# Two transformer layers with mixtures of experts on one core: last experts as riders with late sums, the first part's first four pairs of tiles beside the last convolution, rows and sorts given out sooner

## The chip, the cores and the metric

The kernel runs on one core of a Trainium2 chip, in float32. A core has five engines, each with its own queue of instructions: PE (matrix products), DVE (vector), ACT (scalar with an activation function), POOL (here mostly the issuer of indirect transfers) and SP (issuer of plain transfers). The metric is the device time of one execution, in microseconds (us). The kernel before took 1086.53 us, the median of four runs of 1083.31 to 1088.84.

## The reference

The input x has 4 batches of 1024 rows of 256 features. Two layers follow one another, each of them an attention and a feed-forward part, with a layer norm that is scaled and shifted per batch before both and a gate per batch and feature behind both:

```
h = layernorm(x) * (1 + ca) + sa ;  x = x + ga * attention(h)
h = layernorm(x) * (1 + cb) + sb ;  x = x + gb * feed_forward(h)
```

Layer 0 has a causal softmax attention over a latent of 64 and a feed-forward part of 16 experts, of which each row takes its best two. This change leaves that layer alone. Layer 1 has a linear attention and a feed-forward part of 8 experts:

```
q, k, v = relu(h Wq)+eps, relu(h Wk)+eps, h Wv      # 16 heads of 16, q and k normalised, cubed, normalised
out     = q (k^T v) / (q . sum of k + eps)
y       = out + conv3(out)                          # three taps along the rows, per feature
attention    = y Wproj + b
feed_forward = gate_prob * (h We[e] + be[e]),  e = argmax(h Wr + br)   # one expert for each row
```

## The kernel before

All of x stays on chip. Layer 1 is what matters here.

**attention1** (L1445) walks over b = 0 to 4. In step b it runs `front(b)` beside `back(b-1)`, two generators that are advanced in turn. `front` does the layer norm of batch b, then the products for k and v (L1511), the sums of k and v (ps_kv), and the products for q (L1537). `back` does, for the batch before, the outputs ps_o (L1574), their division by the sums (DVE, L1580), their transposes ps_oT (L1589, copied to `o` by ACT, L1592), the convolution y (one ACT instruction L1597 and two of DVE, L1601, for each half of the features) and the projection ps_pr (L1609, 32 products), which DVE adds to x (L1614). I call these steps stage 0 to stage 4; stage 4 has only `back(3)`.

**Tasks and riders.** `Around` (L34) holds work that is slipped in between. A task is a generator cut into pieces; `step(pieces, rides)` advances the first task by so many pieces and the first rider so many times. A rider is a string of indirect transfers that POOL issues. `attention1` calls `step` after every turn, with a pace of (6, 8, 6, 6, 12) sixths of a piece by stage and one ride. When a stage has ended, `after_batch(b - 1)` appends the tasks of that batch's second half of the layer:

- `rows(b)` (L1827): row statistics, then `routed_rows` (L1017): normalised rows h (ACT, L1030, eight instructions of 128x256; for batches 0 and 1 DVE scales and shifts them, L1045 and L1046), stored to memory (`rows_in`, SP, L1048), transposed (ps_lnT, PE L1057), copied as hT (ACT, L1063 or L1068), and multiplied with the router (L794, L802).
- `sort(p)` (L1846): the best expert of each row, and a counting sort of the rows by expert: ranks on PE (ps_rank, L895), a chain of small DVE instructions, ps_expert (L949), index (L933) and offset (L950). It ends with a new rider, `send(p)` (L1863): rows are fetched (POOL, L1870) and scattered by their index into `sorted1` in memory (POOL, L964).

The rows are sorted in three parts, `PARTS = ((0, 1), (2,), (3,))`: batches 0 and 1 together, then batch 2, then batch 3. An expert's rows are padded to tiles of 128, so the parts have 11, 7 and 7 pairs of tiles.

**Experts1.run** (L1883) walks over these 25 pairs once attention1 has ended. For each it loads two tiles (`xs`, SP L1008, up to five pairs ahead, 256 KB each), transposes them (ps_xT, PE L1923), copies them to `xT` (ACT, L1927 for part 0; for parts 1 and 2 two instructions that also scale and shift, L1930), multiplies with the expert's weights (ps_y, PE L1938, 8 products), adds the bias (DVE, L1944, twice), for parts 1 and 2 multiplies with the gate (DVE, L1946), and stores (`results`, SP L1947). The transposes of a pair are given out ahead of the products of the pair before it. After each pair it calls `step(2, 2)`.

**combine(p)** (L1975) becomes a task when the last pair of its part is given out: it gathers the rows back (`ys`, POOL L974, 128 KB each, six buffers, four ahead), multiplies them with the router's probability and adds them to x: for part 0 with ACT (`out`, L2002), then the gate and the sum on DVE (L2007, L2008); for parts 1 and 2 with one DVE instruction (L1996). Every four tiles a store of 512 KB leaves (L2010).

**Sums.** `count_sums` (L501, four DVE instructions for each of three tensors, L495 to L498) and `out_of_bounds` (L511) check that the attentions' sums were in range, and run before the end of part 1 and of part 2; a general version of the kernel follows behind that check and isn't run here.

**The order of the instructions.** Each engine runs its instructions in the order in which they stand in its queue. Between the points where the program pins that order (`k.pin`), a scheduler chooses it when the kernel is built. ACT's normalised rows (L1030) and outputs of part 0 (L2002) are pinned; the transposes and copies of the experts are not.

Of the kernel before, what the change touches and what calls it, by code (L numbers as in the profile page):

```python
# [15 lines left out]
P = 128  # L16
B, N, C = 4, 1024, 256
NT = N // P
CC = C // P
# [481 lines left out]
def count_sums(k, pool):  # L501

    recs = [k.recs.rearrange("p n i j -> p (n i j)")]
    recs += [k.recs1[:, i].rearrange("p b t h -> p (b t h)") for i in range(2)]
    inverse = 1.0 / SUM_HI, 1.0 / SUM_LO
    for i, (rec, (low, high)) in enumerate(zip(recs, (inverse, (SUM_LO, SUM_HI), inverse))):
        good = pool.tile([P, 8 * B * H], F32, tag="xs", name="good", bufs=6)
        count_within(k, good, rec, low, high, k.good[:, i : i + 1])

# [507 lines left out]
def routed_rows(k, work, b, statistics, scale, shift, wr, br, ne, logits, scalar):  # L1017
# [33 lines left out]
    h = yield from normalised(0)  # L1051
    for q in range(2):
        hT = work.tile([P, CC, 512], F32, tag="hT", name="hT", bufs=1)
        for cc in range(CC):
# [14 lines left out]
            if q == 0 and cc == CC - 1:  # L1069
                h = yield from normalised(1)  # L1070
            else:
                yield 1
# [372 lines left out]
def attention1(ctx, k, a, after_batch=lambda b: None):  # L1445
# [171 lines left out]
    k.misc = ps_m  # L1617
    for b in range(B + 1):
        while b == HB and k.awaited in k.around.tasks:
            k.around.step()  # L1620
        todo = ([front(b)] if b < B else []) + ([back(b - 1)] if b else [])
        pace = (6, 8, 6, 6, 12)[b]
        n = 0
        while todo:
            todo = [g for g in todo if next(g, k) is not k]
            n += pace
            k.around.step(n // 6)
            n %= 6
        if b:
            after_batch(b - 1)  # L1630
# [153 lines left out]
class Experts1:  # L1784


    def __init__(self, k, a, out):
# [19 lines left out]
        self.sent = set()  # L1807
# [74 lines left out]

    def run(self, early):  # L1883

        k = self.k
        nc = k.nc
        work = self.back = self.stack.enter_context(
            k.tc.tile_pool(name="f1_work", bufs=2, reuse_waits="tile")
        )
        ps_x = self.stack.enter_context(  # L1890
            k.tc.tile_pool(name="f1_ps_x", bufs=4, space=PSUM, reuse_waits="tile")
        )
        ps_o = self.stack.enter_context(
            k.tc.tile_pool(name="f1_ps_o", bufs=4, space=PSUM, reuse_waits="tile")
        )
        k.misc = ps_x

        pairs = [
            (p, list(range(g, min(g + 2, s.tiles))))
            for p, s in enumerate(self.sortings)  # L1900
            for g in range(0, s.tiles, 2)
        ]
        coming = []

        def fetch(n):

            for p, tiles in pairs[n + len(coming) : n + 5]:
                if p not in self.sent:
                    break
                xs = work.tile([P, 2, C], F32, tag="xs", name="xs", bufs=6)  # L1910
                k.sorted1[p].load(xs[:, : len(tiles)], tiles)
                coming.append(xs)

        def tiles_of(p, tiles, xs):

            n = len(tiles)
            at = self.sortings[p].offsets(
                self.state[p][1], tiles, [mybir.EngineType.PE, mybir.EngineType.DVE]
            )
            ps = ps_x.tile([P, 2, CC, P], F32, tag="m", name="ps_xT")  # L1920
            for j in range(n):
                for cc in range(CC):
                    nc.tensor.transpose(ps[:, j, cc], xs[:, j, cc * P : (cc + 1) * P], k.ident)  # L1923
            xT = work.tile([P, 2, CC, P], F32, tag="xT", name="xT", bufs=3)
            b = PARTS[p][0] if len(PARTS[p]) == 1 else None
            if b is None:
                nc.scalar.copy(xT[:, :n], ps[:, :n])  # L1927
            else:
                for cc in range(CC):
                    nc.scalar.activation(  # L1930
                        xT[:, :n, cc], ps[:, :n, cc], AF.Identity,
                        bias=k.modF[:, cc, b : b + 1], scale=k.modF[:, 2 + cc, b : b + 1],
                    )
            yield
            po = ps_o.tile([P, 2, C], F32, tag="o", name="ps_y")
            for j in range(n):
                for cc in range(CC):
                    k.anchor = nc.tensor.matmul(  # L1938
                        po[:, j], lhsT=xT[:, j, cc], rhs=self.we[:, cc, bass.ds(at[j], C)],
                        start=cc == 0, stop=cc == CC - 1,  # L1940
                    ).ins
            y = work.tile([P, 2, C], F32, tag="y", name="y", bufs=3)
            for j in range(n):
                nc.vector.tensor_tensor(y[:, j], po[:, j], self.be[:, bass.ds(at[j], C)], ALU.add)  # L1944
            if b is not None:
                nc.vector.tensor_tensor(y[:, :n], y[:, :n], bcast(self.gate[:, b], 1, n), ALU.mult)  # L1946
            nc.sync.dma_start(k.results1[p].part(tiles), y[:, :n])  # L1947

        again, before = None, None
        for n, (p, tiles) in enumerate(pairs):  # L1950
            if p not in self.sent and before is not None:
                next(before, None)
                before = None
            while p not in self.sent:
                k.around.step(1, 2)
            fetch(n)
            now = tiles_of(p, tiles, coming.pop(0))
            next(now)
            if before is not None:
                next(before, None)  # L1960
            before = now
            if n + 1 == len(pairs) or pairs[n + 1][0] != p:
                next(before, None)
                before = None
                if early and p + 2 == len(PARTS):
                    count_sums(k, work)
                if early and p + 1 == len(PARTS):
                    again = out_of_bounds(k, work, ps_x)
                k.around.tasks.append(self.combine(p))
            k.around.step(2, 2)  # L1970
        k.around.drain()
        self.stack.close()
        return again

    def combine(self, p):  # L1975
        k, work = self.k, self.back
        nc = k.nc
        index, _, part = self.state[p]
        most = self.sortings[p].nt

        def fetch(n):
            ys = work.tile([P, C], F32, tag="ys", name="ys", bufs=6)
            self.sortings[p].gather(ys, k.results1[p], index[:, 0, n : n + 1])
            return ys

        coming = []
        for n in range(4):
            coming.append(fetch(n))
            yield 0.5
        for n in range(most):  # L1990
            j = n % 2
            b, t = PARTS[p][n // NT], n % NT
            ys = coming.pop(0)
# [9 lines left out]
            if n + 4 < most:  # L2003
                coming.append(fetch(n + 4))
            if j == 1 and len(PARTS[p]) > 1:
                xs = k.x[b][:, t - 1 : t + 1]
                nc.vector.tensor_tensor(y, y, bcast(self.gate[:, b], 1, 2), ALU.mult)  # L2007
# [10 lines left out]
def two_layers(ctx: ExitStack, tc: tile.TileContext, a: dict, out: bass.AP):  # L2018
# [56 lines left out]
    def stages(first, second, early):  # L2075
# [22 lines left out]
        with ExitStack() as s, tc.using_default_side("right"):  # L2098
# [3 lines left out]
            second(s, k, a, *([after_attention1] if early else []))  # L2102
# [84 lines left out]
```

## The time and the profile before

| | us |
| --- | --- |
| time, median of 4 runs | 1086.53 (1083.31 to 1088.84) |
| the profiled execution | 1090.69, its span 1088.9 |
| PE busy | 951.6 (87%) |
| DVE busy | 620.5 (57%) |
| ACT busy | 602.8 (55%) |
| POOL busy | 336.9 (31%) |
| mean granted clock of PE | 0.950 |

Times within the profile count from the start of the span. The marks that are used below, all from the timeline of PE: the last q product of batch 2 ends at 887.6, that of batch 3 at 939.9; the last ps_pr ends at 972.2; the last ps_y at 1062.7. Layer 1's experts so fill the last 117 of 1088.9 us. In a table by stretches each engine's busy time stands as "busy (xinstructions)"; the two figures behind are the clock that PE was granted, as a share of full speed, the share of the 16 DMA engines' time that is busy, and GB/s. A bracket behind an instruction gives the idle time before it and what ended it.

### The profile page before, as it was taken

How to read it: one execution, taken by the hardware profiler on the slowest of the kernel's cores; microseconds unless marked ns; L12 is line 12 of the kernel's file. 1: busy time of each engine (PE TensorE's matmuls, PEld its weight loads, DVE VectorE, ACT ScalarE, POOL GpSimd, SP SyncE). 2: the span in 40 equal slices, each digit the busy share in tenths (PEclk: the TensorE clock that was granted, in tenths of full speed). 3: DMA queues.
4: the chain of work that ended last, by engine and by line, in shares of the span. 5: the costliest groups of instructions: out<-in, count | busy, mean ns of one | idle time of the engine just before them, and what ended most of it. 6: DMA issues, size and time to landing. Idle time of an engine off the chain costs nothing.

```text
span 1088.9 us, 18090 instructions
## 1 busy us (share of the span) xinstructions
PE 951.6 (87%) x6072; PEld 564.6 (52%) x6072; DVE 620.5 (57%) x1987; ACT 602.8 (55%) x959; POOL 336.9 (31%) x528
## 2 busy tenths in 40 slices
PE   4899999999999999889689999986997989858770
PEld 1434434343443434335567888874465656546650
DVE  5822335422465155414676757993899978664572
ACT  0358754765477555675555666766654745523430
POOL 2013111311222234673004615612550100553632
PEclk9999999999999999999899999998999899989875
DMA  6995000100010001552824656624223201458764
GB/s 196 352 346 192 2 1 6 40 1 1 2 64 1 1 30 54 196 225 75 313 88 163 198 181 187 195 76 144 65 65 148 88 1 39 139 172 258 234 214 129
DMA packets 97142, 132.89 MB, mean 122 GB/s; under 512 B 8536, under 2 KB 84216, under 8 KB 96528
## 3 DMA queue, kind: packets, MB, share of 16 engines
q1 hardware_dynamic: 84656, 97.27, 26.5%
q0 software_dynamic: 11776, 33.57, 9.9%
q8 instruction: 52, 0.85, 0.3%
q10 hardware_dynamic: 608, 0.79, 0.2%
q14 instruction: 50, 0.41, 0.1%
HBM read 67.85 MB, written 63.75 MB: 121 GB/s over the span
## 4 chain that ended last, share of the span: by engine, by line
PE 64%; DVE 18%; DMA 5%; issue 5%; ACT 4%; POOL 1%; SPq 1%; DVEq 0%; ACTq 0%; POOLq 0%
PE ps_s L388 13%; PE ps_av L453 12%; PE ps_qk L364 5%; PE ps_y L1312 5%; PE ps_h L1247 5%; PE ps_v L349 3%; PE ps_out L427 3%; PE ps_pr L1609 3%; PE ps_k L1511 2%; PE ps_q L1537 2%; PE ps_y L1938 2%; DMA ys<-results,index 2%; DVE y L1601 2%; PE ps_lnT L1057 1%; PE ps_xT L1224 1%
## 5 line engine op out<-in xcount | busy, mean ns | idle before, releaser
L396 ACT ACTIVATE pT<-ps_s 128x1024 f32<-128x1024 f32 x288 | 279.3, 1022 | 168.6 <-PE ps_s L388 166.2
L399 POOL TENSOR_SCALAR_AFFINE_SELECT pT<-pT 128x256 f32<-128x256 f32 x256 | 104.0, 430 | 329.7 <-ACT pT L396 325.0
L388 PE MATMUL ps_s<-qT,kT 32*128 32x512 f32 (+3 forms) x1536 | 178.6, 522 | 0.1
L453 PE MATMUL ps_av<-pT,v 128*32 128x512 f32 (+3 forms) x1536 | 166.1, 500 | 8.3 <-DVE turned L411 5.6
L964 POOL DMA_INDIRECT sorted<-hs,index x96 | 97.3, 1013 | 146.1 <-PE ps_y L1312 74.1
L974 POOL DMA_INDIRECT ys<-results,index x96 | 102.8, 1070 | 119.5 <-DMA results<-y 43.6
L388 PEld LDWEIGHTS ps_s<-qT,kT 32*128 32x128 f32 x1536 | 74.3, 184 | 96.0 <-issue 73.4
L453 PEld LDWEIGHTS ps_av<-pT,v 128*32 128x32 f32 x1536 | 40.8, 109 | 103.1 <-issue 59.1
L1247 PE MATMUL ps_h<-w,xT 128*128 x352 | 83.5, 391 | 6.9 <-DVE mv L1259 3.8
L1312 PE MATMUL ps_y<-w,act 128*128 x352 | 84.1, 393 | 4.1 <-DVE rs_seed L84 2.8
L411 DVE STREAM_TRANSPOSE turned<-ps_av 128x512 f32<-128x512 f32 x32 | 22.8, 712 | 97.8 <-PE ps_av L453 97.5
L1247 PEld LDWEIGHTS ps_h<-w,xT 128*128 128x128 f32 x352 | 67.4, 197 | 16.7 <-issue 4.2
L1312 PEld LDWEIGHTS ps_y<-w,act 128*128 128x128 f32 x352 | 67.9, 198 | 14.0 <-ACT act L1295 4.7
L1295 ACT ACTIVATE act<-ps_hT,gain 128x128 f32<-128x128 f32 x176 | 63.6, 462 | 17.0 <-PE ps_hT L1286 17.0
L1270 ACT ACTIVATE hid<-hid,nmr,rstd 128x256 f32<-128x256 f32 x88 | 47.5, 603 | 39.7 <-DVE nmr L1263 39.5
L1938 PE MATMUL ps_y<-we,xT 128*128 x200 | 55.3, 426 | 12.0 <-ACT xT L1930 9.4
L1511 PE MATMUL ps_k<-wqkv,hT 128*128 128x512 f32 x128 | 62.2, 605 | 3.9 <-DMA wqkv<-in_wqkv_dram 3.2
L371 DVE COPY qT<-ps_qk 128x512 f32<-128x512 f32 x16 | 11.0, 690 | 81.3 <-PE ps_qk L364 81.3
L1938 PEld LDWEIGHTS ps_y<-we,xT 128*128 128x128 f32 x200 | 39.7, 211 | 21.8 <-ACT xT L1930 12.2
L103 DVE BATCH_NORM_STATS2 ln_st<-x 128x6 f32<-128x256 f32 x128 | 49.2, 407 | 0.4
L1255 DVE TENSOR_TENSOR hid<-ps_h,b 128x256 f32<-128x256 f32 x88 | 33.9, 415 | 27.4 <-PE ps_h L1247 15.8
L374 DVE TENSOR_SCALAR kT<-ps_qk,par 128x512 f32<-128x512 f32 x32 | 22.5, 745 | 38.1 <-PE ps_qk L364 38.1
(223 smaller groups left out, 1503.0 us busy)
## 6 DMA issues: line engine op xcount, KB each, us to landing
xs<-sorted SPq DMA_DIRECT2D x69, 256.0 KB, 3.7
results<-y SPq DMA_DIRECT2D x69, 256.0 KB, 2.5
sorted<-zero SPq DMA_DIRECT2D x2, 6016.0 KB
rows_in<-h SPq DMA_DIRECT2D x16, 512.0 KB, 4.3
hs<-rows_in POOLq DMA_DIRECT2D x32, 256.0 KB, 3.4
w<-in_w_dram SPq DMA_DIRECT2D x8, 1024.0 KB, 9.8
x<-in_x_dram SPq DMA_DIRECT2D x4, 1024.0 KB, 7.5
b<-in_b_dram SPq DMA_DIRECT2D x2, 2048.0 KB, 16.9
```

The costliest lines, as they stand in the source:

```text
L364: nc.tensor.matmul(ps, lhsT=w[:, cc, g * P : (g + 1) * P], rhs=hT[:, cc, hf * 512 : (hf + 1) * 512], start=cc == 0, stop=cc == CC - 1,)
L388: k.anchor = nc.tensor.matmul(pair[hh // 2][:, hh % 2, c0 : c0 + w], lhsT=kTs[o][rows, kb * P : (kb + 1) * P], rhs=qT[rows, q1 - w : q1], ...
L396: nc.scalar.activation(pT, ps, AF.Exp, scale=1.0 / L**0.5)
L399: nc.gpsimd.affine_select(out=pT[:, :, c0 : c0 + P], in_=pT[:, :, c0 : c0 + P], compare_op=ALU.is_ge, fill=0.0, base=0, pattern=[[0, 2], [ ...
L453: nc.tensor.matmul(po[32 * hh : 32 * hh + 32, 512 - w :], lhsT=vs[b % 2][:, kb, 8 * g + 2 * hh + o, :], rhs=exps[b, g, o, u][hh // 2][:, h ...
L964: i = self.k.nc.gpsimd.indirect_dma_start(out=buffer.ap, out_offset=bass.IndirectOffsetOnAxis(ap=index, axis=0), in_=rows, in_offset=None, ...
L974: self.paced(self.k.nc.gpsimd.indirect_dma_start(out=rows, out_offset=None, in_=buffer.ap, in_offset=bass.IndirectOffsetOnAxis(ap=index, a ...
L1247: mm = nc.tensor.matmul(ph[:, j], lhsT=xTs[i // 2][:, j, cc], rhs=w1[:, cc, bass.ds(at[i + j], C)], start=cc == 0, stop=cc == CC - 1,)
L1295: o = nc.scalar.activation(act[:, j, cc], pt[:, j, cc], AF.Gelu, bias=gain[:, 1, cc, t : t + 1], scale=gain[:, 0, cc, t : t + 1],)
L1312: mm = nc.tensor.matmul(po[:, j], lhsT=acts[i // 2][:, j, cc], rhs=w2[:, cc, bass.ds(at[i + j], C)], start=cc == 0, stop=cc == CC - 1,)
L1511: k.anchor = nc.tensor.matmul(ps, lhsT=hT[:, cc, t * P : (t + 1) * P], rhs=wqkv[:, cc, C:], start=cc == 0, stop=cc == CC - 1,).ins
L1938: k.anchor = nc.tensor.matmul(po[:, j], lhsT=xT[:, j, cc], rhs=self.we[:, cc, bass.ds(at[j], C)], start=cc == 0, stop=cc == CC - 1,).ins
```

## The change

- `attention1` calls `after_batch(b - 1)` when `back(b - 1)` has run out, and no longer at the end of the stage; the pace of stage 3 is 8 for 6; stages 3 and 4 have two rides for each step.
- `routed_rows` normalises both halves of a batch ahead of the first transposes, for batches 2 and 3 (those without `scale`).
- In stage 4 a new call, `fill(turn)`, runs `Experts1.beside`: pairs 0 to 3 of part 0 are fetched from turn 1 on and given out at turns 6, 7 and 8, between the transposes and the convolution and the projection of the last batch. Their buffers are cut from two spare tiles, and their banks of PSUM are the attention's.
- `run` begins at pair 4. It steps four pieces after each pair until part 2 has been sent, then two. The gathers of each part are a rider (`gathers`, with 24 buffers for 6) that is appended as soon as the part's last pair has been given out. `combine(0)` becomes a task when part 1's last pair has been given out; `combine(1)` and `combine(2)` come after all gathers have been issued.
- `count_sums` is given out in three pieces behind pairs 7, 8 and 9, from another buffer; `out_of_bounds` comes behind the last pair.
- The first transpose, the copies and the first product of each pair are pinned, and so is the gate of part 0's outputs.

The core of the diff:

```diff
     for i, (rec, (low, high)) in enumerate(zip(recs, (inverse, (SUM_LO, SUM_HI), inverse))):
-        good = pool.tile([P, 8 * B * H], F32, tag="xs", name="good", bufs=6)
+        good = pool.tile([P, 8 * B * H], F32, tag="out", name="good")
         count_within(k, good, rec, low, high, k.good[:, i : i + 1])
+        yield
...
     h = yield from normalised(0)
+    second = (yield from normalised(1)) if scale is None else None
...
             if q == 0 and cc == CC - 1:
-                h = yield from normalised(1)
+                if second is None:
+                    h = yield from normalised(1)
+                else:
+                    h = second
+                    yield 1
...
-        todo = ([front(b)] if b < B else []) + ([back(b - 1)] if b else [])
-        pace = (6, 8, 6, 6, 12)[b]
+        behind = back(b - 1) if b else None
+        todo = ([front(b)] if b < B else []) + ([behind] if b else [])
+        pace = (6, 8, 6, 8, 12)[b]
         n = 0
+        turn = 0
         while todo:
             todo = [g for g in todo if next(g, k) is not k]
+            if behind is not None and behind not in todo:
+                behind = None
+                after_batch(b - 1)
             n += pace
-            k.around.step(n // 6)
+            k.around.step(n // 6, 1 + b // (B - 1))
             n %= 6
-        if b:
-            after_batch(b - 1)
+            turn += 1
+            if b == B:
+                fill(turn)
...
+    def beside(self, turn):
+        if 0 not in self.sent or turn > 8:
+            return
...
+            self.space, self.most = space, 4
+        self.fetch()
+        for _ in range({6: 2, 7: 1, 8: 1}.get(turn, 0)):
+            self.pair()
+        if turn == 8:
+            self.products()
...
+        while self.done < len(self.pairs):
+            p = self.pairs[self.done][0]
+            if p not in self.sent:
+                self.products()
             while p not in self.sent:
-                k.around.step(1, 2)
...
+                around.step(1, 2)
+            self.pair()
+            if p == 0 and self.done > 6:
+                next(counts, None)
+            if self.done == len(self.pairs) or self.pairs[self.done][0] != p:
+                around.riders.append(self.gathers(p))
+                if p == last - 1:
+                    around.tasks.append(self.combine(0))
+            around.step(2 if last in self.sent else 4, 2)
+        for _ in counts:
+            pass
+        again = out_of_bounds(k, work, ps_x) if early else None
+        while around.riders:
+            around.step(0)
+        around.tasks += [self.combine(p) for p in range(1, last + 1)]
+        around.drain()
...
+    def gathers(self, p):
+        index = self.state[p][0]
+        for n in range(self.sortings[p].nt):
+            ys = self.back.tile([P, C], F32, tag="ys", name="ys", bufs=24)
+            self.sortings[p].gather(ys, self.k.results1[p], index[:, 0, n : n + 1])
+            self.got[p].append(ys)
+            yield
```

As built, the queues of both kernels are the same up to the last q product of batch 1 (at about 830 us). From there on the order on PE is, in the kernel after: in stage 2 the first transposes of `rows(0)` stand beside ps_o of `back(1)`; in stage 3 the ranks of `sort(0)` stand early in the k products, `rows(2)` among the later k and the q products, with the eight h and then the first two hT in one block on ACT, and the ranks of `sort(1)` between the last q product and ps_o of `back(3)`. Stage 4 reads ps_xT 0, ps_xT 1, ps_o, ps_oT, ps_o, ps_oT, ps_y 0, ps_xT 2, ps_y 1, ps_xT 3, ps_y 2, ps_y 3, and then all of ps_pr. Behind it come ps_xT 4, half of `rows(3)`, ps_xT 5, ps_y 4, the other half, ps_xT 6, ps_y 5, the ranks of `sort(2)`, and pairs 6 to 24.

## The prediction, written before the run

> **What bounds the kernel now.** I read the page's head first (PE is busy 87% of the span), then the table by stretches of layer 1, then the chain that ended last, then the waits of ACT and the timelines there. The stretches show where PE's 87% has holes:
>
> ```profile
> core 0: us, PE busy (x) PEld busy (x) DVE busy (x) ACT busy (x) POOL busy (x), PEclk, DMA share, GB/s
> 888.00:909.00 21.00, 15.36 (x92) 10.89 (x91) 15.18 (x28) 13.34 (x23) 0.00 (x0) 0.92 0.14 50
> ...
> 940.00:972.00 32.00, 19.57 (x135) 15.87 (x135) 20.43 (x71) 12.62 (x21) 18.32 (x19) 0.84 0.57 189
> 972.00:997.00 25.00, 20.38 (x135) 15.47 (x134) 11.43 (x52) 10.99 (x20) 8.90 (x11) 1.00 0.74 236
> 997.00:1018.00 21.00, 19.56 (x107) 16.37 (x106) 9.30 (x31) 6.32 (x12) 11.09 (x11) 1.00 0.81 263
> 1018.00:1047.00 29.00, 19.82 (x73) 15.17 (x72) 21.69 (x42) 14.16 (x30) 18.33 (x18) 0.76 0.67 210
> 1047.00:1063.00 16.00, 12.13 (x47) 9.39 (x45) 10.80 (x26) 2.97 (x6) 4.91 (x5) 0.79 0.63 200
> ```
>
> PE is full at 997 to 1018 alone (19.56 of 21 us, full clock). Stage 4 (940 to 972) leaves it 12.4 us idle, the stretch from 1018 to 1047 9.2, and in both the granted clock falls (0.84, 0.76). The chain names who holds it up:
>
> ```profile
> 963.40 8.81 PE ps_pr L1609 x32
> ...
> 1015.56 4.83 DMA ys<-results,index
> 1021.06 3.69 DMA ys<-results,index
> 1024.77 0.51 ACT out L2002
> 1025.28 0.46 ACT xT L1930
> ...
> 1046.71 5.61 DMA xs<-sorted
> ```
>
> The end hangs on part 0's gathers: ACT's queue has `out` (waiting for a gathered tile) ahead of `xT` (which PE waits for). The waits of ACT, and the group of the products with PE's idle time, measure it:
>
> ```profile
> ACT out L2002 <- DMA ys<-results,index: 14.0, 12, 3.0
> ```
>
> ```profile
> L1938 PE MATMUL ps_y<-we,xT 128*128 x56 | 18.8, 490 | 9.2 <-ACT xT L1930 9.2
> ```
>
> The timeline of PE gives the prices: a warm pair, two behind idle time, one with the wait of a sort, one with late rows.
>
> ```profile
> 897.73 0.63 PE L1057 MATMUL ps_lnT<-ident,h 128*128 128x128 f32 x4 [3.60 <-DVE h L1046]
> ...
> 963.19 0.20 PE L949 MATMUL ps_expert<-past,all 8*1 8x14 f32 x2 [7.51 <-DVE index L933]
> ...
> 1016.48 1.89 PE L1938 MATMUL ps_y<-we,xT 128*128 x8
> ...
> 1031.19 2.02 PE L1938 MATMUL ps_y<-we,xT 128*128 x8 [1.75 <-ACT xT L1930]
> ...
> 1052.45 2.02 PE L1923 MATMUL ps_xT<-ident,xs 128*128 128x128 f32 x8 [3.27 <-DMA xs<-sorted]
> 1054.72 3.75 PE L1938 MATMUL ps_y<-we,xT 128*128 x8 [0.25 <-ACT xT L1930]
> ```
>
> A warm pair costs PE 1.73 us (the chain's eight products) + 0.44 (four transposes) = 2.17; between 999 and 1018 pairs follow each other every 2.2 to 2.3.
>
> **The change part by part.** I walk four marks: A, the last q of batch 2 (887.6); B, that of batch 3 (939.9); C, the last ps_pr (972.2); D, the last ps_y (1062.7); then the end, 1088.9.
>
> *Stage 2, A.* `rows(1)`'s PE work moves in from stage 3: 16 transposes, routes and logits, 2.2 us. The second block of four h (2.07 on ACT) and its hT now stand ahead of `back(1)`'s copies o, so convolution and ps_pr come 2.8 later, and one k tile less stands before ps_pr to fill (2.2). Sum +7.2. Bounds: 0 (PE idles before ps_pr anyway) to 7.2, as all three are then open; I take the upper end, since the built order leaves only two k tiles as cover. A = 894.8.
>
> *Stage 3, B.* Away: `rows(1)`'s 2.2, the idle 5.6 of 888 to 909 (3.60 of it the row above), about 1.0 of slow clock (0.92). Added: the ranks of `sort(0)` stand right behind the last q, and ps_expert ahead of half of ps_o, so PE waits for DVE's chain of 18 small instructions: 4.7 in the undisturbed sort (ranks out at 994.4, ps_expert at 999.1) less 1.4 of ps_oT between: 3.3 (bounds 0 and the 7.5 shown). `rows(2)`: 2.7 of PE work; ACT's block of eight h (4.1) and two hT (1.4) is 5.5, of which queued k and q products (1.88 for each tile) hide about half: 2.7 (bounds 0 and 5.5). Sum -8.8 + 3.3 + 5.4 = -0.1; B = 947.0. SP's four early loads of `sorted` stand ahead of batch 2's rows_in and wait for part 0's last scatter. Those scatters start some 9 us behind A, take 31.7 as before (930.1 to 961.8), and a load takes 2.9 + 3.7: 945, so the first ps_xT, which stands ahead of `back(3)`'s ps_o, finds its data 2 us before B. If this cover is gone, PE waits there, us for us. Batch 2's rows leave after that and are needed by scatters only from about 955 on: nothing. Two rides for one cost POOL no time, as each scatter still waits for a product.
>
> *Stage 4, C.* It held 4.1 of `rows(2)` and the 7.5 of ps_expert. Now: two ps_xT and ranks 0.9; chain 4.7 (bounds 0 and 7.5); ps_o, on (0.4 with 0.2 of reciprocal for each of eight) and ps_oT about 8; then pairs 0 to 3 (8.7 on PE), while DVE does the convolution (4 x 1.3) and eight bias sums (0.38 each), 8.3 with the first y: 9.2 together; ps_pr 8.9. Sum 31.7 against 32.3. The pairs so ride where PE idled 12.4 us: free. C = 947.0 + 31.7 = 978.7, +6.5.
>
> *C to D.* Before it took 90.5. Behind ps_pr only pairs 4 and 5 stand among batch 3's rows and sort; 6 to 24 stand behind its ranks. The chain: sum, statistics and reciprocal root 4.1 (972.2 to 976.3); eight h 4.1 and two hT 1.5 on ACT; routes, pair 4, logits 2.8; the other transposes and hT 2.5; routes and pair 5 3.0; then best expert and total 2.4, ranks 0.4, chain 4.7: together 25.5, where before the scatters were released at C + 27.4 with six and a half pairs done. This gives back the early pairs' gain; what the change wins is behind it. Then 12 pairs of parts 0 and 1 by 2.25 = 27.0, and 7 pairs of part 2 by DVE, which now has part 0's sums there: two sums 0.76, gate 0.67, out*gate 0.67 and x+out 0.66 are 2.76; as each starts a little before the one ahead has ended (two sums 0.34 apart at 0.42), 2.5: 17.5 (bounds 2.25 and 2.76). ACT waits for no gather any more: a part's 16 gathers (1.3 each, 21 us) are issued under the seven pairs of the next part and a little beyond, before `out` asks for them; that removes the 14.0 and the 9.2. `count_sums` (2.2 us three times) goes under the two waits for the router; its cost is inside the 2.4 and 4.7.
>
> Clock: two waits of PE here (for h, and for the sort) are each over the 3.27 that left eight products at 3.75 for 1.73: 2 us each, +4 (bounds 0, as the 1.75 wait left 2.02, and 4). The Trainium skill ("TensorE: Matmul & The Clock Gate", section on the HAM clock gate) says that an idle window of about 3.4 us halves the clock, and that about 3.4 us of sustained work regain it. This speaks against the change, which opens two such waits; by it each costs an estimated 1.7, together 3.4 for my 4; the row's 3.27 lies a little under its window.
>
> Transfers: 14 loads and 19 stores of 0.262 MB, 24 gathers and 8 scatters of 0.131, three stores of 0.524 are 14.4 MB in 48.5 us, 297 GB/s. The trace's densest stretch moved 263 at a share of 0.81 while PE waited for none. At 263 it takes 54.8 (+6.3), at 263/0.81 = 325 it hides (0). I take +2.5, as the 263 was met without a wait.
>
> D = 978.7 + 25.5 + 27.0 + 17.5 + 4.0 + 2.5 = 1055.2.
>
> *D to the end.* The last part's way is unchanged: results land, eight gathers by 1.3, 3.9 to land, sum, store: 26.2 as before. `combine(1)` (eight sums of 0.44) fits into the wait for the gathers; were it to stand ahead of the last, 3.5.
>
> The end is 1081.4 against 1088.9: -7.5. The profiled execution took 1090.69, 4.2 above the median of the four runs; I take the difference off the median: 1079.0.
>
> **The rivals.** *Transfers set the tail (the other side).* With the gathers loose and part 0's stores under part 2, everything flows at once. Over C to D before, 20.7 MB moved in 91 us, 228 GB/s. If that is what mixed gathers and loads give, 14.4 MB take 63.2 for 51.0: +12.2, 1091.2. It decides from 246 GB/s downwards (14.4 MB in 58.5 us). For it: the last pairs already waited 3.27 for `xs` at 200 GB/s. Against: those stretches lacked demand, ACT having stopped PE.
>
> *The sorts are dear.* Each of the three ps_expert waits costs 7.5, as the one shown, for 3.3, 4.7 and 4.7, since DVE's queue has reciprocals, convolution or counts between: +9.8, 1088.8. For it: it happened in stage 4. Against: sort(2) took 4.7.
>
> *All that was moved is hidden.* C does not lag (-6.5), the clock holds (-4), transfers hide (-2.5), part 2 goes by PE (-1.75): 1064.2. For it: PE has 5.6 idle us at 888 to 909. Against: the built order, with h in a block on ACT.
>
> That the change doesn't do what it says would leave 1086.5; the built order has all four pairs ahead of ps_pr, and `out` behind part 1, so I give it nothing of its own.
>
> **How the numbers follow.** Main case 0.50 (own range 1072 to 1085: the bounds of ps_expert, clock and transfers), transfers 0.20, sorts 0.15, all hidden 0.15. A measurement of this kernel tells 0.3% (3.3 us) from no change. Faster: 0.48 of the main case, 0.15, and 0.03 of the sorts: 0.66. Same: 0.02 and 0.06: 0.08. Slower: 0.20 and 0.06: 0.26. The range 1065 to 1092 leaves out about half of the chance of the transfers and of the case in which all is hidden, 0.17.
>
> **What would show it.** Right: ps_pr ends 4 to 9 us later than before, with four ps_y ahead of it; ACT's `out` waits for no gather; from the ranks of `sort(2)` on pairs follow every 2.2 to 2.6 us; the last ps_y at about 1055. Wrong: ps_xT 0 waiting for `xs` at B (then part 0's scatters were late); waits for `xs` or `ys` in the tail (transfers); ps_pr later than 985 (sorts or rows not hidden). What I can't see from here is how far DVE's small instructions of a sort are split by others, and what gathers cost loads beside them.

## The result: the same time within 0.2%, and the profile after

The kernel after took 1088.44 us (median of 44 runs, 1082.34 to 1092.24), the kernel before 1086.91 in the same comparisons (70 runs); the ratio is 1.0009, with a 95% interval of 1.0001 to 1.0017. The forecast of 1079.0 is not met. That the time lies inside the range of 1065 to 1092 says little, as that range holds the kernel before too.

The orders of both kernels are the same up to the last q of batch 1, so I count from there (830.2 in the trace before, 826.4 in the one after; these 3.8 us are not of the change). In us behind that mark:

| mark | before | forecast | after |
| --- | --- | --- | --- |
| A, last q of batch 2 | 57.4 | 64.6 | 63.6 |
| B, last q of batch 3 | 109.7 | 116.8 | 118.0 |
| C, last ps_pr | 142.0 | 148.5 | 148.4 |
| ps_expert of batch 3's sort | 168.9 | 174.0 | 177.3 |
| D, last ps_y | 232.5 | 225.0 | 225.8 |
| last y of DVE ready | 234.9 | 227.4 | 232.2 |
| first of the last part's eight gathers | 237.9 | 230.4 | 237.6 |
| end of the span | 258.7 | 251.2 | 258.0 |

Up to the last product the 7.5 us are there within one us (6.7). Behind it they are gone. The table by stretches of the kernel after (busy us, with counts, of PE, PEld, DVE, ACT and POOL, then clock, DMA share and GB/s) covers the same stages:

```profile
944.00:975.00 31.00, 25.59 (x139) 21.76 (x137) 22.17 (x72) 7.86 (x13) 8.04 (x9) 0.94 0.32 103
975.00:1005.00 30.00, 14.56 (x85) 9.70 (x84) 11.97 (x59) 8.83 (x16) 2.95 (x4) 0.75 0.41 131
...
1030.00:1058.00 28.00, 18.85 (x95) 14.23 (x94) 23.80 (x47) 13.04 (x29) 19.97 (x19) 0.95 0.87 277
```

Stage 4 is now full (25.59 of 31, where it was 19.57 of 32). The holes have moved: PE is busy 14.56 of 30 us while batch 3's rows are routed and sorted, at a clock of 0.75, and in the last stretch DVE is the fullest engine (23.80 of 28). The timeline of PE has the waits of the first hole:

```profile
979.39 0.33 PE L1059 MATMUL ps_lnT<-ident,h 128*128 128x128 f32 x1 [4.20 <-ACT h L1031]
...
999.98 0.41 PE L896 MATMUL ps_rank<-sel,before 128*128 128x64 f32 x2 [3.99 <-DVE rtotal L819]
...
1003.68 0.20 PE L950 MATMUL ps_expert<-past,all 8*1 8x14 f32 x2 [3.05 <-DVE index L934]
...
1050.14 2.02 PE L1940 MATMUL ps_y<-we,xT 128*128 x8 [1.41 <-ACT xT L1932]
```

The chain that ended last, in part 2, no longer has a gather in front of `xT`; it is DVE's own queue:

```profile
1045.14 0.76 DVE y L1949 x2
...
1045.92 0.69 DVE y L1951
1046.61 0.54 DVEq L956
...
1047.23 0.70 DVE out L2071
...
1048.57 0.76 DVE y L1949 x2
...
1057.90 0.68 DVE y L1951
1058.60 4.41 DMA results<-y
```

From one pair's bias sums (1045.14) to the next (1048.57) it is 3.43 us: the two sums, the gate, part 0's `out`*gate and x+`out`, and in between a load of a later pair's offsets into DVE's registers (DVEq L956). The six turns from the sums at 1034.33 to those at 1055.70 took 4.49, 3.57, 2.75, 3.43, 2.75 and 4.38 us, 3.56 on average; in the two short ones the load lies under the gate, and the first holds two of part 0's sums. PE needs 2.2 for a pair. The last gated y is done at 1058.6, 6.4 us behind the last ps_y, and the store of the results lands in 4.41. Before, the last y was done 2.4 behind the last ps_y, and the store landed in 2.18 (PE and the chain of the kernel before):

```profile
1059.04 3.62 PE L1938 MATMUL ps_y<-we,xT 128*128 x16
```

```profile
1065.13 2.18 DMA results<-y
```

The waits of ACT in the kernel after no longer hold any for `ys`; what its `out` waits for is DVE, which has to set one of two `out` buffers free:

```profile
ACT out L2068 <- issue: 5.4, 3, 2.0
```

### The profile page after: what moved, and what is told of

Read it like the earlier page. It is cut to its first block, busy times and chain, and to the rows that moved or that the text cites. A ratio compares the mean times of both kernels' runs of the same rounds, so it can differ in the third digit from the quotient of the medians.

```text
span 1084.4 us, 18080 instructions
## 1 busy us (share of the span) xinstructions
PE 943.6 (87%) x6072; PEld 559.3 (52%) x6072; DVE 621.1 (57%) x1987; ACT 601.2 (55%) x959; POOL 336.3 (31%) x528
## 5 line engine op out<-in xcount | busy, mean ns | idle before, releaser
L1301 ACT ACTIVATE act<-ps_hT,gain 128x128 f32<-128x128 f32 x176 | 63.6, 463 | 17.1 <-PE ps_hT L1292 17.1
L103 DVE BATCH_NORM_STATS2 ln_st<-x 128x6 f32<-128x256 f32 x128 | 49.3, 408 | 0.5
L1940 PE MATMUL ps_y<-we,xT 128*128 x168 | 43.0, 404 | 3.4 <-ACT xT L1932 3.4
L1327 DVE TENSOR_TENSOR y<-ps_y,b 128x256 f32<-128x256 f32 x88 | 35.1, 418 | 15.3 <-PE ps_y L1318 15.0
## 6 DMA issues: line engine op xcount, KB each, us to landing
sorted<-zero SPq DMA_DIRECT2D x2, 6016.0 KB, 20.4
```

The lines of the kernel that those rows point to most:

```text
L103: nc.vector.bn_stats(st[:, t, :], k.x[b][:, t, :])
L1301: o = nc.scalar.activation(act[:, j, cc], pt[:, j, cc], AF.Gelu, bias=gain[:, 1, cc, t : t + 1], scale=gain[:, 0, cc, t : t + 1],)
L1940: mm = nc.tensor.matmul(po[:, j], lhsT=xT[:, j, cc], rhs=self.we[:, cc, bass.ds(at[j], C)], start=cc == 0, stop=cc == CC - 1,)
```

## The experiments

I went in with two explanations. **A**: DVE, which carries part 0's sums in part 2, bounds the last pairs and hands out the last results late. **C**: the transfers, with sixteen gathers and three stores of 512 KB among the last pairs, do. **B** was a doubt of the first half: that the early pairs are worth nothing beside what the rows and sorts given out sooner cost.

The runs fall into four comparisons, each on another chip. In the first three the kernel before itself took 1096 to 1099 us, in its one trace there with 9.0 us more ahead of the last q of batch 1 (839.2 for 830.2), so all times there are to be read as ratios to it; in the last comparison it took 1088.21. The kernel after, run as a mark in the second, had a ratio of 1.0058 (1.0029 to 1.0087) there, and in the last 1.0000 (0.9984 to 1.0015).

**Without the early pairs.**

```diff
-            second(s, k, a, *([after_attention1, experts1.beside] if early else []))
+            second(s, k, a, *([after_attention1] if early else []))
```

> The kernel after, without the four pairs in stage 4: all 25 pairs come behind the last ps_pr, as before. Theory A (the early pairs pay; the gain is lost behind the last product, where DVE carries part 0's sums): stage 4 gets about 3 us shorter without them, but only pairs 0 and 1 stand beside batch 3's rows and sort, so four pairs of 2.2 us come on top behind: about 1088.4 - 3 + 8.7 = 1094. Rival B (the early pairs only fill time that batch 3's rows and sort leave open anyway, and the rows and sorts given out sooner are what costs): no slower than the kernel after, 1085 to 1088.

Ratio 1.0140 (1.0102 to 1.0179), about 0.8% above the kernel after. From batch 3's ps_expert to the last ps_y it took 70.9 us (55.9 in the mark of the second comparison, 48.5 in the first trace of the kernel after). By the ratios the four pairs pay some 9 us, so B in its plain form falls. C came 2 us sooner than in the other three kernels of this comparison (148.2 for 150.0 to 150.2), against the 3 us that I expected: without the pairs PE waited 6.1 us for the convolution.

**Part 0's sums behind the last pair.**

```diff
-                if p == last - 1:
-                    around.tasks.append(self.combine(0))
...
-        around.tasks += [self.combine(p) for p in range(1, last + 1)]
+        around.tasks += [self.combine(p) for p in range(last + 1)]
...
-            ys = self.back.tile([P, C], F32, tag="ys", name="ys", bufs=24)
+            ys = self.back.tile([P, C], F32, tag="ys", name="ys", bufs=32)
```

> The kernel after, with combine(0) given out behind the last pair (32 gather buffers for 24), so that DVE and ACT do part 0's sums while the last part's results land and are gathered. Theory A: in part 2 DVE has 1.43 us for a pair instead of 2.8 and the register loads, pairs follow every 2.2 instead of 2.9 us, and the last gated y comes about 2.4 us behind the last product instead of 6.4: the last results leave some 8 us sooner; the tail behind them (21.5 us) then also holds 11 us of DVE work and three more stores of 512 KB, which fit: 1080 to 1083. Rival C (transfers set the end): the stores only move behind, the same bytes have to pass, 1087 to 1091. Rival B: no change, 1088.

Ratio 1.0053 (1.0013 to 1.0093): no gain. Of A's mechanism one half shows: DVE is ready 1.5 us behind the last product (6.0 in the mark of the second comparison, 6.4 in the first trace). The other half, that PE is done sooner, does not: from ps_expert to the last product it took 57.5 us (55.9 in that mark), as PE waited 4.29 us for `xT` in the stall that is looked at below; behind it the last pairs do follow every 2.2 us. And A had left something out: from the first of the last gathers to the end it now takes 24.9 us, and 20.4 to 21.6 in all other kernels but this one. The timelines of DVE and of SP's queue in this kernel:

```profile
1071.53 0.69 DVE L1951 TENSOR_TENSOR y<-y,gate_f 128x512 f32<-128x512 f32 x1
```

```profile
1076.07 17.91 SPq L2072 DMA_DIRECT2D out_dram<-x  x8
```

All eight stores of x now stand in the tail, where the kernel after has five. Moved work was paid for where it went.

**Two pieces after each pair.**

```diff
-            around.step(2 if last in self.sent else 4, 2)
+            around.step(2, 2)
```

> The kernel after, with two pieces of a task after each pair instead of four while part 2 hasn't been sent. In the built order pairs 4 to 8 then stand among batch 3's rows and sort, instead of 4 and 5 alone. Where those waits of PE are what is open (it was busy 14.6 of 30 us there), three pairs of 2.2 us go for nothing and the sort ends 1 to 2 us later: 1083 to 1085. If the transfers set the end (rival C): 1087 to 1089.

Ratio 1.0114 (1.0062 to 1.0167): slower, for a reason that I hadn't seen. With fewer pieces the sort of part 2 ends after part 0's last pair, its rider comes behind part 0's gathers, and PE waits for the scattered rows (PE, then POOL's first scatter, which follows the last of sixteen gathers):

```profile
1064.96 1.94 PE L1923 MATMUL ps_xT<-ident,xs 128*128 128x128 f32 x8 [24.36 <-DMA xs<-sorted]
```

```profile
1050.40 1.04 POOL L965 DMA_INDIRECT sorted<-hs,index  x1 [0.30 <-issue]
```

So this run says nothing on the open waits of PE; the kernel with the scatters first, below, asks again.

**Without the gate of parts 1 and 2.**

```diff
-        if b is not None:
-            nc.vector.tensor_tensor(y[:, :n], y[:, :n], bcast(self.gate[:, b], 1, n), ALU.mult)
```

> The kernel after, without the multiplication by the gate for parts 1 and 2 (batches 2 and 3 so lack the gate on their experts), which takes one DVE instruction of 0.69 us off each of 14 pairs and leaves every transfer and the order of all else. Theory A (DVE bounds part 2, and holds the last results): part 2's pairs at 2.2 to 2.3 us instead of 2.9, the last y about 2 us behind the last product instead of 6.4: 1079 to 1083. Rival C (transfers bound it): no change, 1087 to 1089.

Ratio 1.0013 (0.9985 to 1.0040), below the 1.0058 of the kernel after in the next comparison: less work on DVE, with the same bytes, is faster, as far as two comparisons can be set beside each other (their intervals overlap a little). The last y comes 1.2 us behind the last product, and the first of the last gathers 5.7 (10.9 in that mark, 5.4 before). All eight stores of x stay, three of them in part 2 (1055.69, 1060.81 and 1065.31 in SP's queue), and near the end DVE waits for PE again (PE, then DVE):

```profile
1065.43 3.62 PE L1940 MATMUL ps_y<-we,xT 128*128 x16
```

```profile
1065.50 0.76 DVE L1949 TENSOR_TENSOR y<-ps_y,be 128x256 f32<-128x256 f32 x2 [0.22 <-PE ps_y L1940]
```

So the lag behind the last product is DVE's work, and no transfer's. The end is not as early as A had it; from ps_expert to the last product it took 54.7, with a stall of 5 us that is looked at below.

**The last part of the change alone.**

```diff
-    second = (yield from normalised(1)) if scale is None else None
+    second = None
...
-        pace = (6, 8, 6, 8, 12)[b]
+        pace = (6, 8, 6, 6, 12)[b]
...
-            if behind is not None and behind not in todo:
-                behind = None
-                after_batch(b - 1)
...
-            k.around.step(n // 6, 1 + b // (B - 1))
+            k.around.step(n // 6)
...
-            if b == B:
-                fill(turn)
+        if b:
+            after_batch(b - 1)
```

> The kernel after once more, unchanged, as the mark beside which the three others are read: within 0.3% of the kernel before on the same chip.

> Only the last part of the change: attention1 and routed_rows as in the kernel before (tasks given out at the end of each stage, pace 6, one ride, halves normalised one after the other, no pairs in stage 4), and Experts1.run as in the kernel after (gathers as riders, part 0's sums under part 2, four pieces). If the rows and sorts given out sooner cost what C showed (the last ps_pr 6.4 us later against the last q of batch 1) and the early pairs return it, this is as fast as the kernel after: C 6 us sooner, and three pairs of 2.2 us more behind the sort of batch 3, ratio to before 0.997 to 1.004. If the early pairs are worth more than their stages' lag: slower than the kernel after by 0.5% or more. If they are worth nothing: 0.5% faster than before.

Ratio 1.0059 (1.0023 to 1.0096) against 1.0058 for the kernel after in the same comparison. C is back at 142.2, where it was before the change (142.0; 150.2 in the kernel after here). So in this comparison the stages' lag costs what the four early pairs bring. That the stages' changes and the early pairs cancel is the first of the outcomes that I had written down, though the ratio itself lies above the 1.004 that went with it, as does the mark's.

**Six buffers for y.**

```diff
-            [P, 2, C], F32, tag=name, name=name, bufs=6 if name == "xs" else 3
+            [P, 2, C], F32, tag=name, name=name, bufs={"xs": 6, "y": 6}.get(name, 3)
```

> The kernel after with six buffers for the experts' outputs y instead of three. Theory D (the results' stores land in 3 to 5 us among the gathers, and DVE waits for one of three buffers, so that it falls behind PE): DVE's waits for the landing of results vanish, part 2's pairs follow every 2.5 us, the last y comes 3 to 4 us sooner: ratio 0.3% under the kernel after. Theory A (DVE's own work of 2.8 us for each pair with part 0's sums is what bounds): no change, as it has no time to spare.

Ratio 1.0046 (1.0017 to 1.0075): not told apart from the kernel after. DVE's one wait for a store of results (2.9 us) is gone, but the last y still comes 6.0 us behind the last product. The buffers are not what holds DVE.

**Two pieces, with the scatters ahead of the gathers.**

```diff
-        k.around.riders.append(self.send(p, index))
+        k.around.riders.insert(0, self.send(p, index))
...
-            around.step(2 if last in self.sent else 4, 2)
+            around.step(2, 2)
```

> The kernel of two pieces after each pair, with the rider of a part's scatters put ahead of the gathers that wait already. If what slowed the kernel of two pieces was alone that part 2's eight scatters stood behind part 0's sixteen gathers on POOL (PE then waited 24.4 us for xs): that wait goes, pairs 4 to 8 stand under batch 3's rows and sort, and it is 0.3 to 0.6% faster than the kernel after. If pairs among the rows delay the sort by as much as they take, it is the same as the kernel after.

Ratio 0.9955 (0.9927 to 0.9984): faster than both kernels, by 1.0% than the kernel after beside it. Pairs 4 to 8 now stand among batch 3's rows (PE busy us in the first column behind the length):

```profile
990.00:1020.00 30.00, 21.48 (x121) 16.23 (x119) 17.99 (x74) 10.70 (x19) 2.95 (x4) 0.83 0.56 177
```

PE is busy 21.48 of those 30 us, where it was 14.56 in the like stretch of the first trace, and from ps_expert on 43.6 us are left to the last product instead of 55.9. Three more pairs ahead of the sort's end are some 6.6 of these 12.3 us; the stall of PE that is shown below for the mark (4.64 us) is absent here, and how much of the gain is which isn't shown. Of the last part's DVE lag nothing has changed (11.5 us from the last product to the first of the last gathers).

**The kernel before again, half of the gathers, one piece, and the last part with the scatters first** ran in one comparison.

> The kernel before once more, unchanged, for its trace on the chip of the next three: the same marks as in its first trace, counted from the last q of batch 1 (last ps_pr +142.0, last ps_y +232.5, end +258.7). If the stall of 5 to 7 us at the beginning of part 2, which the kernel after and most of its variants show on this chip, is one of the kernel after, it isn't here; if it comes from elsewhere, it is.

The marks are those of its first trace (C 142.2, last ps_y 233.2, end 259.3).

```diff
-            ys = self.back.tile([P, C], F32, tag="ys", name="ys", bufs=24)
-            self.sortings[p].gather(ys, self.k.results1[p], index[:, 0, n : n + 1])
+            if p or n % 2 == 0:
+                ys = self.back.tile([P, C], F32, tag="ys", name="ys", bufs=24)
+                self.sortings[p].gather(ys, self.k.results1[p], index[:, 0, n : n + 1])
```

> The kernel after with half of part 0's gathers left out (a gathered tile is used for two tiles of rows, so every second tile of batches 0 and 1 gets another tile's experts): 8 gathers of 128 KB less on POOL and on the DMA engines; each instruction of PE, ACT, DVE and SP stays. Theory C (from the first gathers of part 0 on the transfers bound the tail, at a DMA share near 1): the wait at the beginning of part 2 shrinks or goes, part 2 gets 3 to 6 us shorter, ratio about 0.4% under the kernel after. Theory A (DVE's work with part 0's sums bounds part 2): no change.

Ratio 1.0005 (0.9969 to 1.0041). By itself this speaks for C, though its interval overlaps with the mark's of the second comparison. In that mark all DMA engines are busy at the beginning of part 2, and PE has nothing from ACT for 4.64 us (a stretch, then PE):

```profile
1041.00:1044.00 3.00, 1.12 (x6) 0.64 (x4) 1.75 (x4) 0.00 (x0) 2.08 (x4) 1.00 1.05 370
```

```profile
1046.77 3.78 PE L1940 MATMUL ps_y<-we,xT 128*128 x8 [4.64 <-issue]
```

With half of the gathers that stall is absent, and ps_expert to last product takes 49.3 for 55.9; the lag behind the last product stays at 11.8, as it must if that is DVE's. The stall is not tied to the kernel after alone: ACT has a wait of 5 to 8 us of this kind in nine of the twelve traces of the first three comparisons, the kernel before's among them, and in none of the last comparison or of the first two traces.

```diff
-            around.step(2, 2)
+            around.step(1 if p == last else 2, 2)
```

> The kernel with two pieces and the scatters put first, with one piece instead of two after each pair of part 2, so that seven of part 0's sixteen sums stand under part 2 and nine behind it. Theory A: the last y follows the last product 3 us sooner, and the tail has room: 2 to 3 us faster than with two pieces. Theory C: the stores of part 0 move into the tail and lengthen it by as much: the same.

This edit is made to the kernel with the scatters first. Ratio 0.9973 (0.9949 to 0.9997), not told apart from two pieces (0.9955 in the comparison before). The lag behind the last product shrinks from 5.6 to 3.6 us and the time behind the first of the last gathers grows from 20.7 to 21.6.

> The kernel that has only the last part of the change, with two pieces after each pair and the scatters put ahead of the gathers. Pairs 0 to 3 then stand under batch 3's rows and sort, 21 behind. If early pairs and the rows and sorts given out sooner are worth nothing together, as the comparison of the kernel after with the last part alone has it: as fast as the kernel with all of the change, two pieces and scatters first (0.995 of before). If the early pairs pay once the rest flows: 0.5 to 1% slower than that one.

Both edits of the kernel with the scatters first, made to the one that has the last part alone. Ratio 1.0112 (1.0077 to 1.0147), 1.6% (some 17 us) above the kernel with all of the change and the same two edits. That alone doesn't show that the early pairs pay here: PE waited 11.1 us once for `xs`, and that wait comes from this kernel's own edit. Part 1's scatters, put first, go ahead of the last two of part 0, for whose rows PE waits behind the last ps_pr (PE, then POOL's fifteenth scatter, which batch 2's sort released):

```profile
993.84 1.11 PE L1919 MATMUL ps_xT<-ident,xs 128*128 128x128 f32 x4 [11.10 <-DMA xs<-sorted]
```

```profile
974.09 1.01 POOL L965 DMA_INDIRECT sorted<-hs,index  x1 [1.40 <-DVE mine L948]
```

**Without part 0's sums on DVE.** To see both explanations at once, I took DVE's part away without moving it. It was meant to leave every transfer in place; it does not, as the traces show.

```diff
-                k.pin(nc.vector.tensor_tensor(y, y, bcast(self.gate[:, b], 1, 2), ALU.mult))
-                nc.vector.tensor_tensor(xs, xs, y, ALU.add)
```

> The kernel after, unchanged, as the mark for the two that follow, in the same comparison: 0 to 0.6% above the kernel before.

> The kernel after without the two DVE instructions (out*gate, x+out) of part 0's eight sums, so that batches 0 and 1 leave without their last experts: 11 us of DVE work less in part 2, moved nowhere; every transfer, and ACT's out, stay. Theory A: from the last product to the first gather of the last part 6 us as in the kernel before (5.4) instead of 11 to 12, part 2's pairs every 2.2 to 2.3 us: 0.6 to 0.9% under the kernel after. Theory C alone (transfers): the last product no sooner and the last results held by the DMA engines: under 0.2%.

Ratio 0.9935 (0.9912 to 0.9957), 1080.41 us, against 1.0000 (0.9984 to 1.0015) of the kernel after. Here are PE, DVE and POOL of the mark, and then PE, DVE, POOL and the first stores of x of the kernel without sums:

```profile
1054.02 2.02 PE L1940 MATMUL ps_y<-we,xT 128*128 x8 [1.42 <-ACT xT L1932]
```

```profile
1061.73 0.69 DVE L1951 TENSOR_TENSOR y<-y,gate_f 128x512 f32<-128x512 f32 x1
```

```profile
1067.64 0.99 POOL L975 DMA_INDIRECT ys<-results,index  x1 [7.80 <-DMA out_dram<-x]
```

```profile
1045.30 3.62 PE L1940 MATMUL ps_y<-we,xT 128*128 x16
```

```profile
1050.87 0.69 DVE L1951 TENSOR_TENSOR y<-y,gate_f 128x512 f32<-128x512 f32 x1
```

```profile
1056.80 1.00 POOL L975 DMA_INDIRECT ys<-results,index  x1 [1.48 <-PEq L2176]
```

```profile
812.66 5.59 SPq L2072 DMA_DIRECT2D out_dram<-x  x2
864.01 3.56 SPq L2072 DMA_DIRECT2D out_dram<-x  x2
```

The last product ends 3.0 us sooner against the last q of batch 1 (221.8 for 224.8), the last y 2.6 behind it for 6.4, the first of the last gathers 7.9 behind it for 11.6; the end is at 250.3 for 257.1. But without the sums nothing holds the four stores of batches 0 and 1 back: they leave at 812.66 and 864.01, where the mark has three of them in part 2 (1043.44, 1049.11, 1055.30) and one behind its last y. So this run takes DVE's sums and 2 MB of stores out of the end together, and does not tell A from C by itself; what tells them apart for the lag is the run without the gate. For the 3.0 us of PE there is only the chain, in which ACT's xT stand behind `out`, and `out` behind DVE. That the end comes so near to the 251.2 of the forecast is partly luck: D is 3.2 us sooner than forecast, and the time behind it is 28.5 us for the 26.2 of the forecast.

```diff
-            ys = self.back.tile([P, C], F32, tag="ys", name="ys", bufs=24)
-            self.sortings[p].gather(ys, self.k.results1[p], index[:, 0, n : n + 1])
+            if p or n % 2 == 0:
+                ys = self.back.tile([P, C], F32, tag="ys", name="ys", bufs=24)
+                self.sortings[p].gather(ys, self.k.results1[p], index[:, 0, n : n + 1])
```

> The same, and half of part 0's gathers left out too (a gathered tile is used twice). If DVE's work alone took the forecast gain: the same as without the sums. If DVE's work and the gathers' traffic each took part of it: 0.3 to 0.5% under the kernel without sums, and about 0.7% under the kernel before, which is what was forecast.

Ratio 0.9932 (0.9910 to 0.9954), 1080.42 us: the same. Eight gathers less bring nothing once the sums and those stores are gone, so in this condition C falls as far as the gathers go; the stores alone were not tested. What the stall at the beginning of part 2 was in the second comparison, where half of the gathers did seem to help, stays open: the profile puts ACT's wait there down to a queue that it doesn't know, and a wait of that kind (5.4 us, of ACT) is in the second trace of the kernel before too, where it costs the end nothing.

## Why the prediction was wrong, step by step

- *Stage 2, A.* +7.2 forecast, +6.2 measured. The size holds within 1 us, the reason only in part: PE waits 11.72 us ahead of the first transposes of `rows(0)`, which now stand ahead of ps_o, where before it waited 2.00, 0.32 and 5.72 with ps_o in between.
- *Stage 3, B.* -0.1 forecast, +2.1 measured. The wait at ps_expert was 2.82 (3.3 taken), but the ranks in front of it waited another 1.84 for the best expert, and some work of `rows(2)` was less hidden than taken. The loads of part 0 were there in time: no wait of ps_xT 0.
- *Stage 4, C.* -0.6 forecast, -1.9 measured, with all four pairs inside. C was forecast at +6.5 and came at +6.4, by luck in part, as the misses of the three stages (-1.0, +2.2, -1.3) cancel.
- *C to D.* 76.5 forecast, 77.4 measured. Inside, the rows and sort took 28.9 to ps_expert, for 25.5; with the clock term of 4 us for the two waits that is close, and the waits are the 4.20 and 3.99 shown. Eight products behind the first took 3.71 us, behind the second (and the 3.05 of ps_expert) 2.87 (1.73 warm). The Trainium skill ("TensorE: Matmul & The Clock Gate", section on the HAM clock gate) has its threshold at about 3.4 us of idle time; both waits lie above it, so this trace agrees with it; the 3.27 of the kernel before, a little under it, had left eight products at 3.75 as well.
- *Part 2 on DVE: the term that was mis-sized.* I took 2.5 us for each of seven pairs, bounds 2.25 and 2.76, from the four kinds of instruction alone. It is 3.56 on average, 2.75 to 4.49 (the six turns above). On top come the register loads of the experts' offsets, 2.6 us of the chain in these six turns (0.26, 0.67, 0.54, 0.92, 0.23), seven of part 0's sums where I had six (1.4 more), and 0.35 to 0.43 in front of five of the bias sums, where the chain names no wait; none of these is in my sum. ACT's `out` is not among them: DVE sets its buffers free, and ACT waits. PE was held by it only in part (20.4 us for 17.5, a pair every 2.9 us where I had named 2.2 to 2.6 as the sign), which is why D hardly shows it.
- *D to the end: the step that failed.* "The last part's way is unchanged ... 26.2 as before" is wrong. It took 32.2: DVE was 4.0 us further behind PE than before, and the results' store landed 2.2 later. I had moved DVE's sums into part 2 in one sentence and asked only whether PE would be slowed, not how far behind PE DVE would be when PE ends. The run without the gate shows the first of the two to be DVE's work: there the last y is 1.2 us behind PE. The 2.2 of the store stay open: from the last y to the first of the last gathers it is 3.0 us before, and 4.5, 5.2 and 5.1 in the kernels without the gate, without the sums, and without the sums and half of the gathers.
- *The rivals.* Transfers as the tail's limit was given 0.20 and its price 12.2. The gathers' traffic costs nothing in the last comparison, in the kernel without the sums; what the stores cost is not shown. The sorts, given 0.15, were not dear: the three waits at ps_expert were 2.82, 3.17 and 3.05, where that rival had 7.5 for each. The wait for gathers, on the other hand, did go: the 14.0 of ACT all of it, and of the 9.2 of PE for `xT` 3.4 are left.

The Trainium skill (same page, section on the array's architecture, at the depths of the engines' queues) states that ACT and DVE work through their queues strictly in order. The trace shows what that does here: the second last pair's bias sums start at 1055.70, though PE had done all products by 1052.16, because part 0's sums stand ahead of them.

## What to carry to other kernels

When an engine gets work that used to lie elsewhere, add up its time per turn of the loop, waits for registers and buffers included, and compare it with the turn of the engine that sets the pace. If it is longer, the difference times the turns holds the pace-setter up in part, and the rest is a lag that the last engine in line pays after the pace-setter has ended, where the marks of the pace-setter don't show it. Moving the work behind the end was no cure here, as its transfers went with it; filling waits that are open anyway (PE's, during the last sort) is what the two kernels that beat the kernel before with all of its work have in common (0.9955 and 0.9973).

## What I had not expected

- DVE's loads of the offsets into registers, one for each pair of tiles, stand in the chain with 0.2 to 0.9 us each, except in the two of six turns in which the gate covers them.
- An edit that takes instructions away can free a transfer that waited for them: without part 0's sums, four stores of 512 KB left some 190 to 230 us ahead of where they stood.
- Three stores of 512 KB and eleven us of DVE work, moved behind the last pair, lengthened the tail from 20.4 to 24.9 us.
- A queue of riders in the order in which they were appended let 16 gathers pass ahead of 8 scatters: 24.4 us of waiting from one change of a step count.
